# Two ends of a depthwise-convolution stage, and results kept in DRAM by block of channels

## The chip, the cores and the metric

The kernel runs on one core of a Trainium2 chip. The core has five engines that run side by side and meet through semaphores: TensorE (PE, matrix products into PSUM), VectorE (DVE), ScalarE (ACT), GpSimd (POOL) and SyncE (SP), whose work here is to issue DMAs. ScalarE and GpSimd issue DMAs too. The metric is the device time of one execution in microseconds. Every engine takes its instructions in the order in which they stand in its queue, so an instruction that waits holds up all that stand behind it.

## The reference

Two layers follow each other on x of 32 images, 96 channels and 56 by 56 pixels, in float32:

```python
# layer 0
h = conv_general_dilated(x, conv_w, (1, 1), ((3, 3), (3, 3)), feature_group_count=96) + conv_b   # 7 x 7
h = (h - mean_c(h)) * rsqrt(var_c(h) + 1e-5) * ln_g + ln_b        # over the 96 channels
h = gelu(h @ w1 + b1) @ w2 + b2                                    # 96 -> 384 -> 96
x = h * layer_scale + x
# layer 1
x = silu(conv_general_dilated(x, conv_w, (1, 1), ((2, 2), (2, 2)), feature_group_count=96) + conv_b)  # 5 x 5
dts, Bs, Cs = x_proj_w @ x
delta = softplus(dt_w @ dts + dt_b)
P = exp(cumsum(maximum(delta * A, log 1e-9)))                      # A = -exp(A_logs), along the 3136 pixels
y = sum_n(P * cumsum(delta * Bs * x / maximum(P, 1e-9)) * Cs) + x * Ds
```

## The kernel before

The work falls into four stages that follow each other: the 7x7 convolution with the sums for the norm (lines 181 to 481), the MLP (487 to 589), the 5x5 convolution (596 to 683) and the scan (691 to 972). Between stages the results lie in DRAM.

**First convolution.** There are 48 jobs of TensorE work (line 185). The first 40 take two channels each, both halves of the image rows; the last eight take four channels of one half each, four jobs for the lower half (40 to 43) and four for the upper (44 to 47). A job has an x tile of four loads (`load_x`, 224 KB each), a tile of taps of four loads (`load_taps`, from a padded table `taps1_d` in DRAM), a matrix made from the taps by one ScalarE copy (`turn`), 128 products in two PSUM tiles (`convolve`), the eviction with the bias on ScalarE and the store to `conv1_d` by ScalarE's queue (`evict`), and sums and sums of squares for the norm on VectorE, with the square on ScalarE (`add_sums`). Four x tiles, four taps tiles, three matrices, three result tiles and four PSUM tiles are in turn.

The loop at line 453 sets the order. In round n, x and taps of job n+3 are asked for, job n is convolved and evicted, its sums begin, the matrix of job n+2 is turned, and the squares of job n-1 are summed. Calls that go through `pin` keep the order of the program on their engine; calls without it are placed by a scheduler. Before, the x and taps loads and the loads of rows aren't pinned, and the scheduler has put the taps on SP two jobs ahead of the x rows (taps of job n+2 stand before x of job n). From round 2 on, one entry of the list `beside` (line 345) is done per round: `first_weights` (w1 is scaled by ln_g and centred by a product into a PSUM tile, and the bias by three more), `first_rows` four times (VectorE copies the product out of PSUM to four quarters of `w1r_t`, three copies each), `second_weights`, `scan_weights`, `scan_rows`, `turn_taps` and `second_taps` four times, the last of which stores the second convolution's table `taps2_d` by SP's queue.

In job 44 the norm of the lower half is finished (`finish_norm`: sums on VectorE, square root on ScalarE, reciprocal on VectorE) and stored to `rstd_d` by GpSimd's queue.

**MLP.** Its 28 groups are four image rows of one half of the images each. `load_rows` brings three tiles h of 128 partitions (four rows times 32 channels) by four loads each, 32 partitions per load, and a tile r (the reciprocals, the same for all channels) by four loads, all by SP's queue. `normalise` multiplies h by r on VectorE. `hidden` and `result` are the two products, with the GELU on ScalarE between them and the sum with x on VectorE after them. A finished tile of four rows and 32 channels goes to `block_d` by four stores of GpSimd's queue (line 563). `load_rows` for the first two groups is called in the convolution's round 45 (line 479).

**Second convolution.** For each of 96 channels, `load_channel` brings a tile of taps and two tiles of 120 partitions from `block_d` (30 rows times four pieces of 480 values), by SP's queue. Sixteen products per half, a SiLU on ScalarE and four copies (three on VectorE, line 660) follow, and the store to `conv2_d`.

Every DMA of the built program takes one of eight completion semaphores of its kind in turn (eight for SP and ScalarE together, eight for GpSimd), and waits until the previous DMA on that semaphore has landed.

Of the kernel before, what the change touches and what calls it, by code (L numbers as in the profile page):

```python
# [8 lines left out]
F32 = mybir.dt.float32  # L9
# [40 lines left out]
def convnext_then_scan_kernel(  # L50
# [29 lines left out]

    conv1_d = [dram.tile([128, C, HALF], F32, name=f"conv1_{h}_d") for h in range(2)]
    block_d = dram.tile([C, H, QC, B2, BI * QP], F32, name="block_d")
    conv2_d = dram.tile([C, H, B * W], F32, name="conv2_d")
    du_d = dram.tile([B * NCH, C, 2, CH], F32, name="du_d")
    rstd_d = [dram.tile([128, HALF], F32, name=f"rstd_{h}_d") for h in range(2)]
# [23 lines left out]
    def two(t):  # L111
        return t.rearrange("p (s q) -> p s q", s=2)
# [44 lines left out]
    def load_rows(n):  # L157
        h, row, p = group(n)
        for d in range(blocks):
            ht = inputs.tile([128, COLS], F32, name=f"h_{n}_{d}", tag="h", bufs=9)  # L160
            for i in range(RB):
                nc.sync.dma_start(
                    two(ht[CB * i : CB * i + CB]),
                    conv1_d[h].rearrange("(p s m) c q -> p m c s q", s=2, m=RW)[
                        p, row + i, CB * d : CB * d + CB
                    ],
                )
            hts[n, d] = ht
        rt = inputs.tile([128, COLS], F32, name=f"r_{n}", tag="r")
        rts[n] = rt  # L170
        for i in range(RB):
            at = rstd_d[h][2 * RW * p + row + i, 0:1]
            nc.sync.dma_start(
                two(rt[CB * i : CB * i + CB]),
                bass.AP(at.tensor, at.offset, [[0, CB], [RW * HALF, 2], [1, HALF]]),
            )
# [4 lines left out]
    with tc.tile_pool(name="prep", bufs=1) as prep, tc.tile_pool(name="c1", bufs=4) as pool, tc.tile_pool(  # L181
# [14 lines left out]
        def load_x(n):  # L196
            xts[n] = pool.tile([128, 2 * COLS], F32, name=f"xt1_{n}", tag="xt")
            for k, (c, h) in enumerate(jobs[n]):
                nc.sync.dma_start(
                    two(xts[n][RW * k : RW * k + RW]),  # L200
                    x[c].rearrange("(j m) q -> m j q", m=H)[h * (H - RW) : h * (H - RW) + RW],
                )

        load_x(0)

# [19 lines left out]
        for t in acc1, acc2:  # L225
            nc.vector.memset(t, 0.0)

        c2b_t = across(c2b, 128, C, "c2b_t", const)
        dtb_t = column(dtb, C, "dtb_t", const)
        g_t = column(ln_g, C, "g_t")  # L230
        lnb_t = column(ln_b, C, "lnb_t")
        b2_t = column(b2, C, "b2_t")
        ls_t = column(ls, C, "ls_t")
        ls_b = across(ls, 128, C, "ls_b")
        ds_t = column(ds, C, "ds_t")
        w1_t = prep.tile([C, F], F32, name="w1_t")
        nc.gpsimd.dma_start(w1_t, w1)
        b1_t = prep.tile([128, 3], F32, name="b1_t")
        nc.gpsimd.dma_start(b1_t, b1.rearrange("(f p) -> p f", p=128))
        nc.gpsimd.dma_start(w2_t, w2.rearrange("(f p) c -> p f c", p=128))  # L240
# [28 lines left out]
        def second_taps(k):  # L269

            for f in range(QC):
                for t in range(2):
                    j = 4 * t + (k if k < 2 else k - 4) - f + K2 // 2
                    if j in range(K2):
                        kept(nc.vector.tensor_copy,
                            pad2[:, k, RW - K2 : RW, f * 2 + t], turned[:, :, j]
                        )
            if k == QC - 1:
                nc.sync.dma_start(taps2_d, pad2)

        w1g = prep.tile([C, F], F32, name="w1g")
        held: dict = {}
# [1 line left out]
        def first_weights():  # L284

            cen = prep.tile([C, C], F32, name="cen")
            kept(nc.vector.tensor_scalar, cen, ident[:C, :C], -1.0 / C, None, ALU.add)
            kept(nc.vector.tensor_scalar, w1g, w1_t, g_t, None, ALU.mult)
            held["w1"] = bank("ps_w1")[:, 0]
            nc.tensor.matmul(held["w1"][:C, :F], lhsT=cen, rhs=w1g, start=True, stop=True)  # L290
            ps = bank("ps_b1")[:, 0]
            for f in range(3):
                nc.tensor.matmul(
                    ps[:, f : f + 1], lhsT=w1_t[:, f * 128 : (f + 1) * 128], rhs=lnb_t,
                    start=True, stop=True,
                )
            kept(nc.vector.tensor_add, b1p_t, ps[:, :3], b1_t)
# [44 lines left out]
                sel_t, ident.rearrange("p (d n) -> p d n", n=N), mybir.AxisListType.X, ALU.add  # L342
            )

        beside = [first_weights] + [lambda i=i: first_rows(i) for i in range(RB)]
        beside += [second_weights, scan_weights, scan_rows, turn_taps]
        beside += [lambda k=k: second_taps(k) for k in range(QC)]

        def load_taps(n):

            wt = pool.tile([128, RW * K1], F32, name=f"wt1_{n}", tag="wt")
            for k, (c, h) in enumerate(jobs[n]):
                at = taps1_d[c, (1 - h) * R1 * K1 : (1 - h) * R1 * K1 + 1]
                (nc.sync if n else nc.scalar).dma_start(
                    wt[RW * k : RW * k + RW],
                    bass.AP(at.tensor, at.offset, [[K1, RW], [1, RW * K1]]),
                )
            wts[n] = wt

        def turn(n):  # L360
# [31 lines left out]
        def evict(n, pss):  # L392
            job = jobs[n]
            hs = (
                pool_o.tile([128, JT, HALF], F32, name=f"hs1_{n}", tag="hs")
                if n
                else pool_o.tile([128, JT, HALF], F32, name="first", bufs=1)
            )
            c, h = jobs[n][0]
            for a in range(2):  # L400

                parts = (
                    [(hs.rearrange("p (h a) q -> p a h q", h=2)[:, a], pss[a][:, :, :HALF], c + a)]
                    if n < whole
                    else [(hs[:, 2 * a + k], pss[a][:, k, :HALF], c + 2 * a + k) for k in range(2)]
                )
                for to, ps, ch in parts:
                    pin(nc.scalar.activation(  # L408
                        to, ps, AF.Identity, bias=c1b_t[:, ch : ch + 1], scale=1.0
                    ))  # L410
            for g in range(2) if n < whole else [h]:
                cs = slice(c, c + 2) if n < whole else slice(c, c + JT)
                of = slice(2 * g, 2 * g + 2) if n < whole else slice(0, JT)
                pin(nc.scalar.dma_start(conv1_d[g][:, cs], hs[:, of]))
            return hs

        def add_sums(n, hs):
# [28 lines left out]
        for n in range(1, 3):  # L446
            load_x(n)
            load_taps(n)
        for n in range(2):
            turn(n)  # L450
        upper = whole + len(jobs[whole:]) // 2
        squares = None
        for n in range(len(jobs)):
            if n + 3 < len(jobs):
                load_x(n + 3)
                load_taps(n + 3)
            pss = convolve(n)
            norm = finish_norm(0) if n == upper else iter(())
            next(norm, None)
            hs = evict(n, pss)  # L460
            next(norm, None)
            if n == 0:
                first = hs
            if n == len(jobs) - 2:
                for d in range(blocks):
                    normalise(0, d)
            before, squares = squares, add_sums(n, hs)
            next(norm, None)
            if n + 2 < len(jobs):
# [12 lines left out]

# [4 lines left out]
    with tc.tile_pool(name="mlp_g", bufs=14) as pool_g, tc.tile_pool(  # L487
# [47 lines left out]
        def result(n, s, d):  # L535
# [24 lines left out]
                ))  # L560
            if p == 1 and s == 1:
                m = (1 - h) * QR + row
                for i in range(RB):
                    nc.gpsimd.dma_start(  # L564
                        block_d[CB * d : CB * d + CB, m + i].rearrange("c k j q -> c (k j q)"),
                        ot[CB * i : CB * i + CB].rearrange("p k q -> p (k q)"),
                    )

        parts = groups * 2
        norm = finish_norm(1)  # L570
# [25 lines left out]
    with tc.tile_pool(name="c2", bufs=3) as pool, tc.tile_pool(  # L596
# [13 lines left out]
        def load_channel(c):  # L610
# [406 lines left out]
```

## Time and profile before

| | |
|---|---|
| median of three runs | 3349.66 us (3343.58 to 3350.96) |
| profiled execution, whole | 3343.99 us |
| its span, first to last instruction | 3342.2 us |
| busy: PE, DVE, ACT, POOL | 2775.9, 2599.4, 2241.5, 1686.6 us |
| first product of the first convolution | 17.90 us |
| first product of the MLP | 387.18 us |
| first product of the second convolution | 1220.20 us |
| first product of the scan | 1572.0 us |
| DMA | 788.08 MB, 303,130 packets, mean 236 GB/s |

The span is that of one profiled execution; all times in views of the trace count from its first instruction. A row of the timeline gives start, duration, engine, source line, operation, tile written and tile read, shape and number of instructions taken together; in brackets stands how long the engine had been idle and whose end released it. "SPq" and "ACTq" rows are DMAs being issued, not DMA work. In the page's slices the span is cut in 40 parts of 83.6 us, each digit a busy share in tenths. A table of windows gives, for a stretch, the busy time of each engine, TensorE's granted clock, the busy share of the 16 DMA engines and GB/s.

### The profile page before, as it was taken

What the parts mean: (1) busy time and instruction counts of PE and PEld (TensorE: products, weight loads), DVE (VectorE), ACT (ScalarE), POOL (GpSimd) and SP (SyncE); (2) the same over time, 40 slices, a digit from 0 to 9 for tenths busy, and PEclk for the clock granted to TensorE, in tenths of its full rate; (3) what the DMA queues carried; (4) which work ended last, traced back from release to release, by engine and by line L of the source; (5) the groups of instructions that cost most, each with busy time, mean ns of one, the idle gap of its engine ahead of it and who ended that gap; (6) DMA issues with size and microseconds to landing.
All of it is one profiled execution on the core that took longest, in us unless ns stands there. A gap on an engine that the chain in (4) does not pass through costs nothing. (4 is left out here: it accounts for less than half of the span.)

```text
span 3342.2 us, 54129 instructions
## 1 busy us (share of the span) xinstructions
PE 2775.9 (83%) x21898; PEld 1064.9 (32%) x21898; DVE 2599.4 (78%) x1538; ACT 2241.5 (67%) x1963; POOL 1686.6 (50%) x815
## 2 busy tenths in 40 slices
PE   5999899999999989997677777777777777777775
PEld 2566433333333333343222222222222222222221
DVE  4888743333333349997799999999999999999998
ACT  3566543333333348786888887888888888878784
POOL 1000101010010100000899898989899998989896
PEclk8999899999999999998666666666666666666767
DMA  7899856555565459998887877878787878778773
GB/s 188 262 304 293 237 152 182 149 166 163 150 183 145 129 142 278 285 289 226 293 296 246 284 258 272 261 271 277 257 280 248 291 250 283 255 273 264 269 267 113
DMA packets 303130, 788.08 MB, mean 236 GB/s; under 512 B 125680, under 2 KB 195952, under 8 KB 278336
## 3 DMA queue, kind: packets, MB, share of 16 engines
q1 hardware_dynamic: 266832, 659.81, 62.9%
q10 hardware_dynamic: 27200, 82.59, 6.6%
q0 software_dynamic: 8848, 42.23, 4.5%
q8 instruction: 172, 2.82, 0.4%
q14 instruction: 78, 0.64, 0.1%
HBM read 543.58 MB, written 240.90 MB: 235 GB/s over the span
## 5 line engine op out<-in xcount | busy, mean ns | idle before, releaser
L815 POOL TENSOR_TENSOR rep<-rep,bt 128x1568 f32<-128x1568 f32 x192 | 674.5, 3513 | 380.4 <-DMA rep<-du_d 380.4
L844 POOL TENSOR_TENSOR hs<-hs,ct 128x1568 f32<-128x1568 f32 x191 | 669.4, 3505 | 98.6 <-DVE hs L832 87.2
L825 DVE TENSOR_TENSOR_SCAN pv<-rep,pv 128x1568 f32<-128x1568 f32 x192 | 664.4, 3461 | 40.0 <-ACT rep L811 23.0
L530 ACT ACTIVATE g<-ph,b1p_t 128x896 f32<-128x896 f32 x336 | 319.9, 1003 | 483.0 <-PE ph L520 483.0
L553 DVE SCALAR_TENSOR_TENSOR o<-po,b2r_t,x 128x224 f32<-128x224 f32 x336 | 190.8, 609 | 529.9 <-PE po L539 523.1
L564 POOL DMA_DIRECT2D block_d<-o x168 | 81.2, 490 | 727.5 <-DVE o L553 622.4
L520 PE MATMUL ph<-h,w1r_t 32*128 32x448 f32 x4032 | 430.2, 554 | 5.9 <-ACT hs L408 4.2
L743 PE MATMUL pz<-xs,wd_t 96*96 96x392 f32 x512 | 275.3, 703 | 172.6 <-ACT du L751 128.0
L539 PE MATMUL po<-g,w_t 128*32 128x448 f32 x4032 | 413.0, 543 | 0.0
L862 PE MATMUL py<-hs,sel_t 128*32 128x392 f32 x1536 | 324.9, 673 | 61.8 <-POOL hs L844 61.6
L790 PE MATMUL pk<-bn,pick_t 8*128 8x392 f32 x1024 | 289.0, 685 | 93.5 <-ACT y L871 80.4
L828 DVE SCALAR_TENSOR_TENSOR pv<-pv,rep 128x1568 f32<-128x1568 f32 x192 | 345.6, 1800 | 21.7 <-POOL rep L815 1.8
L380 PE MATMUL ps<-xt,mat 32*64 32x432 f32 (+2 forms) x6144 | 320.9, 564 | 45.2 <-ACT mat L362 38.4
L832 DVE TENSOR_TENSOR_SCAN hs<-rep,carry_h,pv 128x1568 f32<-128x1568 f32 x96 | 334.1, 3480 | 10.0
L660 DVE COPY st<-yt 28x896 f32<-28x896 f32 x288 | 323.3, 1123 | 22.7 <-ACT yt L651 12.7
L637 PE MATMUL ps<-xq,wt 128*32 128x448 f32 x3072 | 307.2, 546 | 38.6 <-DMA xq<-block_d 29.3
L832 DVE TENSOR_TENSOR_SCAN hs<-rep,pv 128x1568 f32<-128x1568 f32 x96 | 328.4, 3420 | 9.6
L810 ACT ACTIVATE rep<-rep,lift_t 128x1568 f32<-128x1568 f32 x192 | 307.6, 1602 | 6.2
L811 ACT ACTIVATE rep<-rep,lift_t 128x1568 f32<-128x1568 f32 x192 | 307.6, 1602 | 6.3
L809 ACT ACTIVATE rep<-rep,a_t 128x1568 f32<-128x1568 f32 x192 | 308.3, 1606 | 1.8 <-DMA rep<-du_d 1.4
L854 PE MATMUL py<-xs,dsm_t 96*96 96x392 f32 x512 | 299.7, 726 | 10.0 <-ACT ct L794 4.5
L520 PEld LDWEIGHTS ph<-h,w1r_t 32*128 32x128 f32 x4032 | 192.3, 185 | 245.5 <-issue 153.0
(110 smaller groups left out, 2795.6 us busy)
## 6 DMA issues: line engine op xcount, KB each, us to landing
rep<-du_d SPq DMA_DIRECT2D x191, 1568.0 KB, 8.2
du_d<-du SPq DMA_DIRECT2D x126, 588.0 KB, 9.2
xq<-block_d SPq DMA_DIRECT2D x192, 225.0 KB, 5.1
xt<-in_x_dram SPq DMA_DIRECT2D x192, 224.0 KB, 4.6
block_d<-o POOLq DMA_DIRECT2D x168, 240.0 KB, 4.9
h<-conv_d SPq DMA_DIRECT2D x336, 112.0 KB, 2.6
x<-in_x_dram SPq DMA_DIRECT2D x336, 112.0 KB, 2.5
conv_d<-st SPq DMA_DIRECT2D x96, 392.0 KB
```

The source lines that it names most:

```text
L380: nc.tensor.matmul(pss[k // 2][2 * RW * p : 2 * RW * p + 2 * RW, k % 2, :HALF].rearrange("p (i r) -> p i r", r=W2)[:, :, lo:hi], lhsT=wv[r ...
L520: pin(nc.tensor.matmul(phs[i // 2][:, i % 2, :HALF], lhsT=w1r_t[rows, d, f * 128 : (f + 1) * 128], rhs=hts[n, d][rows, s * HALF : (s + 1) ...
L530: pin(nc.scalar.activation(gt, ph[:, :, :HALF], AF.Gelu, bias=b1p_t[:, f : f + 1], scale=1.0))
L539: pin(nc.tensor.matmul(po[CB * i : CB * i + CB, :HALF], lhsT=w2_t[:, f, CB * d : CB * d + CB], rhs=gts[n, s, f, i // 2][:, i % 2], start=( ...
L660: pin(copy(st[:, :, :, :, f], yt[RW * f : RW * f + QR].rearrange("p h (b q) -> p h b q", q=QW),))
L809: pin(nc.scalar.activation(da, da, AF.Exp, scale=a_t[:, g : g + 1]))
L815: pin(nc.gpsimd.tensor_mul(ut, ut, bts[i // NG]))
L825: pin(nc.vector.tensor_tensor_scan(grown, da, zero, pv[:, last : last + 1] if q else 1.0 / EPS, ALU.mult, ALU.add))
L828: pin(nc.vector.scalar_tensor_tensor(run, in0=grown, scalar=1.0, in1=ut, op0=ALU.min, op1=ALU.mult))
L832: pin(nc.vector.tensor_tensor_scan(ht, da, run, carry_h[:, col : col + 1] if q else 0.0, ALU.mult, ALU.add))
L844: pin(nc.gpsimd.tensor_mul(ht, ht, cts[k]))
L862: pin(nc.tensor.matmul(py[g * DG : (g + 1) * DG, s, :BK], lhsT=sel_t, rhs=hss[k * NG + g][:, cols], start=False, stop=True, tile_position= ...
```

## The change

1. **w1 first.** `first_weights` and `first_rows` leave the list `beside` and are called before job 0, between the first and the second matrix. The loads they need (w1, ln_g, ln_b, b1) move to the front of GpSimd's queue, ahead of the other small loads. The product and the bias share one PSUM tile. The entries left in `beside` come five rounds earlier.
2. **Taps behind their rows.** The loads of x and of taps are pinned, so that SP has x of a job and then its taps. The taps of job 0 go by SP's queue instead of ScalarE's.
3. **The other end.** The store of `taps2_d` goes by GpSimd's queue instead of SP's. `load_rows` of the first two groups is called in rounds 44 and 45, and their r loads go by GpSimd's queue.
4. **Layout.** `conv1_d` and `block_d` are laid out by blocks of 32 channels, so that the four rows of a tile h, and the four rows of a finished block, are one contiguous piece: one load where four were, and one store where four were. The channel's loads in the second convolution then read 30 pieces of 7,680 bytes that lie 245,760 bytes apart, in place of one contiguous piece.

```diff
-    conv1_d = [dram.tile([128, C, HALF], F32, name=f"conv1_{h}_d") for h in range(2)]
-    block_d = dram.tile([C, H, QC, B2, BI * QP], F32, name="block_d")
+    conv1_d = [dram.tile([C // CB, 128, CB, HALF], F32, name=f"conv1_{h}_d") for h in range(2)]
+    block_d = dram.tile([C // CB, H, CB, QC * B * QP], F32, name="block_d")
...
-            for i in range(RB):
-                nc.sync.dma_start(
-                    two(ht[CB * i : CB * i + CB]),
-                    conv1_d[h].rearrange("(p s m) c q -> p m c s q", s=2, m=RW)[
-                        p, row + i, CB * d : CB * d + CB
-                    ],
-                )
+            rows = conv1_d[h][d].rearrange("(p s m) c q -> p (m c) s q", s=2, m=RW)
+            nc.sync.dma_start(two(ht), rows[p, CB * row : CB * (row + RB)])
...
-            nc.sync.dma_start(
+            (nc.sync if n >= 2 else nc.gpsimd).dma_start(
                 two(rt[CB * i : CB * i + CB]),
...
-                nc.sync.dma_start(
+                pin(nc.sync.dma_start(
                     two(xts[n][RW * k : RW * k + RW]),
...
-        c2b_t = across(c2b, 128, C, "c2b_t", const)
-        dtb_t = column(dtb, C, "dtb_t", const)
+        w1_t = prep.tile([C, F], F32, name="w1_t")
+        nc.gpsimd.dma_start(w1_t, w1)
         g_t = column(ln_g, C, "g_t")
         lnb_t = column(ln_b, C, "lnb_t")
+        b1_t = prep.tile([128, 3], F32, name="b1_t")
+        nc.gpsimd.dma_start(b1_t, b1.rearrange("(f p) -> p f", p=128))
...
-                nc.sync.dma_start(taps2_d, pad2)
+                nc.gpsimd.dma_start(taps2_d, pad2)
...
-            held["w1"] = bank("ps_w1")[:, 0]
+            ps = bank("ps_w1")
+            held["w1"], ps = ps[:, 0], ps[:, 1]
...
-        beside = [first_weights] + [lambda i=i: first_rows(i) for i in range(RB)]
-        beside += [second_weights, scan_weights, scan_rows, turn_taps]
+        beside = [second_weights, scan_weights, scan_rows, turn_taps]
...
-                (nc.sync if n else nc.scalar).dma_start(
+                pin(nc.sync.dma_start(
                     wt[RW * k : RW * k + RW],
...
-                cs = slice(c, c + 2) if n < whole else slice(c, c + JT)
+                d, at = divmod(c, CB)
+                cs = slice(at, at + 2) if n < whole else slice(at, at + JT)
                 of = slice(2 * g, 2 * g + 2) if n < whole else slice(0, JT)
-                pin(nc.scalar.dma_start(conv1_d[g][:, cs], hs[:, of]))
+                pin(nc.scalar.dma_start(conv1_d[g][d][:, cs], hs[:, of]))
...
-        for n in range(2):
-            turn(n)
+        turn(0)
+        first_weights()
+        for i in range(RB):
+            first_rows(i)
+        turn(1)
...
-            if n == len(jobs) - 3:
-                load_rows(0)
-                load_rows(1)
+            if n in (upper, upper + 1):
+                load_rows(n - upper)
...
-                for i in range(RB):
-                    nc.gpsimd.dma_start(
-                        block_d[CB * d : CB * d + CB, m + i].rearrange("c k j q -> c (k j q)"),
-                        ot[CB * i : CB * i + CB].rearrange("p k q -> p (k q)"),
-                    )
+                nc.gpsimd.dma_start(
+                    block_d[d, m : m + RB].rearrange("m c q -> (m c) q"),
+                    ot.rearrange("p k q -> p (k q)"),
+                )
...
-                rows = block_d[c, (H - RW + 2) * (1 - h) : (H - RW + 2) * (1 - h) + RW - 2]
+                first = (H - RW + 2) * (1 - h)
+                rows = block_d[c // CB, first : first + RW - 2, c % CB]
                 pin(nc.sync.dma_start(
                     xqs[c % len(xqs)][h][2 * QC * h : 2 * QC * h + (RW - 2) * QC],
-                    rows.rearrange("m k j q -> (m k) (j q)"),
+                    rows.rearrange("m (k q) -> m k q", k=QC),
                 ))
```

More of the change, by code (lines that the diff above doesn't have):

```diff
@@ L198, in load_x @@
             for k, (c, h) in enumerate(jobs[n]):
-                nc.sync.dma_start(
+                pin(nc.sync.dma_start(
                     two(xts[n][RW * k : RW * k + RW]),
                     x[c].rearrange("(j m) q -> m j q", m=H)[h * (H - RW) : h * (H - RW) + RW],
-                )
+                ))
         load_x(0)
@@ L234, in convnext_then_scan_kernel @@
         ls_b = across(ls, 128, C, "ls_b")
+        nc.gpsimd.dma_start(w2_t, w2.rearrange("(f p) c -> p f c", p=128))
+        c2b_t = across(c2b, 128, C, "c2b_t", const)
+        dtb_t = column(dtb, C, "dtb_t", const)
         ds_t = column(ds, C, "ds_t")
[L236 to L240, printed above, removed]
         xp_t = prep.tile([R, C], F32, name="xp_t")
@@ L288, in first_weights @@
             kept(nc.vector.tensor_scalar, w1g, w1_t, g_t, None, ALU.mult)
-            held["w1"] = bank("ps_w1")[:, 0]
+            ps = bank("ps_w1")
+            held["w1"], ps = ps[:, 0], ps[:, 1]
             nc.tensor.matmul(held["w1"][:C, :F], lhsT=cen, rhs=w1g, start=True, stop=True)
-            ps = bank("ps_b1")[:, 0]
             for f in range(3):
@@ L353, in load_taps @@
                 at = taps1_d[c, (1 - h) * R1 * K1 : (1 - h) * R1 * K1 + 1]
-                (nc.sync if n else nc.scalar).dma_start(
+                pin(nc.sync.dma_start(
                     wt[RW * k : RW * k + RW],
                     bass.AP(at.tensor, at.offset, [[K1, RW], [1, RW * K1]]),
-                )
+                ))
             wts[n] = wt
@@ L562, in result @@
                 m = (1 - h) * QR + row
-                for i in range(RB):
-                    nc.gpsimd.dma_start(
-                        block_d[CB * d : CB * d + CB, m + i].rearrange("c k j q -> c (k j q)"),
-                        ot[CB * i : CB * i + CB].rearrange("p k q -> p (k q)"),
-                    )
+                nc.gpsimd.dma_start(
+                    block_d[d, m : m + RB].rearrange("m c q -> (m c) q"),
+                    ot.rearrange("p k q -> p (k q)"),
+                )
         parts = groups * 2
```

## The prediction

> **What bounds the kernel now.** I read the page's slices first, then the table of windows at the stage borders, then TensorE's timeline in the first stage and ScalarE's at its end. The chain of what ended last lies in the scan alone (VectorE 6%, GpSimd 4%), so it says nothing of the stages that change.
>
> ```profile
> PE   5999899999999989997677777777777777777775
> DMA  7899856555565459998887877878787878778773
> ```
> ```profile
> 200.00:260.00 60.00, 59.84 (x1216) 43.43 (x1208) 57.07 (x29) 36.60 (x37) 0.00 (x0) 1.00 1.00 303
> 355.00:388.00 33.00, 18.75 (x260) 9.68 (x264) 25.96 (x24) 12.81 (x19) 0.55 (x1) 0.77 0.78 245
> 388.00:1209.00 821.00, 819.28 (x8064) 305.88 (x8056) 283.93 (x428) 327.38 (x342) 86.64 (x168) 1.00 0.53 153
> 1209.00:1558.00 349.00, 307.32 (x3076) 132.15 (x3072) 325.27 (x295) 273.64 (x193) 3.35 (x7) 0.98 0.93 279
> ```
>
> The columns of the second block are stretch, length, busy us of PE, weight loads, VectorE, ScalarE and GpSimd, then clock, DMA share and GB/s. In its best stretch (200 to 260) the first convolution has TensorE, VectorE and DMA full together: 9.4 jobs of 6.36 us at 303 GB/s. The MLP (388 to 1209) is TensorE without gaps. The second convolution is VectorE's copies (320.5 of 349 us) with DMA at 0.93. So only the first stage has time to give, at its two ends:
>
> ```profile
> 17.90 20.48 PE L380 MATMUL ps<-xt,mat 32*64 32x448 f32 x384 [17.90 <-ACT mat L362]
> 52.41 1.56 PE L290 MATMUL ps_w<-w1g,cen 96*96 96x384 f32 x2 [14.04 <-DVE w1g L259]
> 54.98 9.04 PE L380 MATMUL ps<-xt,mat 32*64 32x448 f32 x132
> 96.22 4.15 PE L380 MATMUL ps<-xt,mat 32*64 32x448 f32 x48 [2.45 <-DVE w1r_t L259]
> ...
> 361.53 8.66 PE L380 MATMUL ps<-xt,mat 32*64 32x448 f32 x128 [6.71 <-ACT mat L362]
> 373.71 9.28 PE L380 MATMUL ps<-xt,mat 32*64 32x448 f32 x128 [3.52 <-ACT mat L362]
> 387.18 6.34 PE L520 MATMUL ph<-h,w1r_t 32*128 32x448 f32 x28 [4.19 <-ACT hs L408]
> ```
> ```profile
> 15.95 1.28 ACT L362 ACT_TABLE_LOAD   x1 [15.95 <-DMA wt<-taps_d]
> ...
> 359.02 1.28 ACT L139 ACT_TABLE_LOAD   x1 [4.55 <-DMA h<-conv_d]
> 373.06 0.59 ACT L362 COPY mat<-wt 128x224 f32<-128x224 f32 x1 [9.48 <-DMA r<-rstd_d]
> ```
>
> The brackets hold the idle time before a row and what ended it. TensorE idles 63.4 us before 388: 17.9 until the first taps land, 14.0 for the folded w1, 6.1 more in jobs 4 to 8, 0.7 at job 10, 6.2 in jobs 19 to 24, 4.0 in jobs 35 to 41, 14.4 in the last two jobs and at the MLP's start. At the end ScalarE, in order, sits with its conv1 store: each DMA takes one of eight completion semaphores in turn and waits for that semaphore's previous owner, here the 19 small h loads and the r loads that wait for the norm.
>
> **What the Trainium skill says.** "DMA: Bandwidth & Descriptors", section "Issuing engines are not separate DMA queues": a transfer runs on the same 16 engines whichever queue issues it. The trace agrees: the stage stops at 303 GB/s with SP and ScalarE both issuing, so moving a store to GpSimd frees the queue, not bandwidth. The same page, "Latency and other measured facts", lists HBM row pitches: 512 KiB at full rate, 2 MiB and more slower; the new pitches here are 56 and 240 KiB, and no run here shows them. "TensorE: Matmul & The Clock Gate", section "What's actually happening": an array left idle restarts at half clock for some 3.4 us. The trace agrees: jobs after a long gap take 9.04, 8.66 and 9.28 us against 6.36, so such a gap costs about 2.5 us beyond itself.
>
> **The change, part by part.**
>
> *Head.* The job-0 taps load leaves ScalarE's queue for SP's, behind four x rows rather than beside eight. Its store has landed at 7.5 us in both (SP's and ScalarE's waits end at 7.6). Four issues take 1.8 us (the row at 7.60), and with 0.9 MB instead of 1.8 MB ahead I take 2.7 us for landing (this line's loads: 1.8 least, 4.9 median): 12.0. Table load 1.28 and copy 0.60 follow: first matmul at 13.9, **-4.0** (0 if the landing stays slow, -5 at best). The wait is new to SP: from about 2.9 to 7.6 it stands before those taps, with x of jobs 1 and 2 behind; x of job 1 then lands by some 15, and job 1 needs it at 20.7. The w1 load needs to come before that: GpSimd issues it, g, ln_b and b1 right after the memsets, at about 3.3 to 5.6; an early small load took 4.7 us (c2b, 3.27 to 8.0). So w1g is made near 9, the matmuls (2.6 us) end near 12 under the wait for the taps, and twelve copies (6.6 us) end before job 0's sums need VectorE at 22. Without that cover they cost at most 2.6. Gone: the gap **-14.0**, its 2.6 us of matmuls **-2.6**.
>
> *Held PSUM bank.* The w1 bank no longer takes one of four tiles through jobs 3 to 8: 0.38+1.08+1.07+1.10+2.45 = **-6.1**. Two slow restarts go with the gaps, 9.04 to 6.5 and 8.0 to 6.5: **-4.0**. The other weight work moves five jobs earlier, and the loads now have no pause to catch up in. VectorE has 6.1 of 6.36 us filled per job and gets 6.9 us of small copies in eight jobs; buffers for two jobs cover it. For all that I give back **+3** (0 to 9).
>
> *Order of x and taps.* Before, taps ran two jobs ahead of x on SP; now they follow their own rows. Counted from the end of job n: the store of n lands at about +6.7 (1.9 evict, 4 to 5 to land), releases the last taps DMA of job n+4, which lands by +10 to +12; ScalarE wants it at about +15 and TensorE at +19.1, three jobs on. Cover is some 4 us, so cost 0; if it goes, every job pays the excess.
>
> *Taps of the second convolution to GpSimd; h in one load.* SP stood 5.0 us for that table at 149 to 154, with x and taps behind it; then came the h loads, and TensorE lost 6.2 us plus 1.8 of slow restart (8.15 us at 160). On GpSimd the store waits for VectorE's last copy, and behind it stands only the rstd store of job 44. The bytes stay (0.79 + 0.46 MB, 4 us at 303 GB/s), so **-5** of 8 (-1 to -8). At jobs 35 to 41 the h load holds one semaphore, not four: **-1.5** of 4.0.
>
> *Tail.* From the end of job 43 (342.1): sums and norm finish on VectorE at +15.7. ScalarE's store of job 44 now waits only for a taps load, so sqrt and the next tap matrix end at +17, not +19.4. Job 46 runs 8.66 to +25.7; the store of job 45 waits for the fifth h load, about +24 (3.2 MB of h and 0.9 of store from +12, at 270 GB/s), and the last tap matrix is ready before +25.7, so job 47 follows at once and ends at +32.2. rstd lands at about +25, the four r loads now on GpSimd at about +30, and VectorE's three multiplications end at +33. Behind these r loads GpSimd has only the five block memsets, which wait for VectorE's last sums anyway (393.6 before). Evicting job 47 (2.2) opens the MLP at +34.5 instead of +45.1: **-10.6** (-4 to -14).
>
> *Stores of the blocks, channel loads.* 168 GpSimd issues of 0.49 us become 42, on an idle engine under TensorE's MLP: nothing. At the last block, three issues less (1.4 us) before the 11.04 us wait, with the same bytes on DMA: **-1** (-2 to +1). The channel loads keep 1,920-byte packets, 240 per channel, now from 7,680-byte pieces 240 KiB apart: 0.
>
> Sum: -4.0-14.0-2.6-6.1-4.0+3.0-5.0-1.5-10.6-1.0 = **-45.8**. Against the profiled execution's 3343.99 (span 3342.2) that is 3298.2; the runs' median, 3349.66, stands 5.7 higher, their lowest beside the profile. Between, I forecast **3301 us**. DMA as a check: to the end of job 45 some 93 MB pass, 2 MB by 13 us; at 300 GB/s that is 316, and my sum puts that end at 354.8-34.2 = 320.6. It fits, barely.
>
> **Rivals.**
> 1. *DMA or late taps set the pace.* For: share 1.00 at 303 GB/s, taps cover of only 4 us. Against: 200 to 260 ran without gaps. At +0.4 us in 44 jobs, 18 us come back: **3319**.
> 2. *Nearly every gap closes.* All 63.4 idle less 13.9, plus 8 of restarts and 2.6: -60, so **3287**. Against: the norm's own chain (4 us) stays.
> 3. *Slower: the channel loads by strided pieces.* Its place is the second convolution, at 0.93 DMA share. A channel there takes 3.48 us and about 3.2 of DMA work by the trace's packets (1,920 bytes: 111 ns). It decides when a channel takes 0.48 us more, which is 0.76 more of DMA work, packets of 162 ns. At 190 ns (1.19 us more work, 0.28 of it hidden) the stage grows by 87 us: 3301+87 = **3388**. Against: size and count stay, and the pitch is half of one the skill lists at full rate.
> 4. *The w1 work is not early.* If w1's load lands after the taps, job 0 waits behind it in TensorE's order; even landing at 14.8, as before, it leaves a 3 us later start: **3304**.
>
> **How the numbers follow.** Forecast and rival 4: 0.66; rival 1: 0.17; rival 2: 0.08; rival 3: 0.06, of which 0.05 end slower; no net change by a mixture: 0.03. A measurement tells about 0.2% (7 us) from none. So faster 0.92, same 0.03, slower 0.05. The low end is rival 2 (3286), the high end rival 1 with the head's and tail's poor bounds (3326).
>
> **What would show it.** First convolution matmul near 14, w1's two matmuls before it; no gap at jobs 2 to 8; no SP pause for the second taps; job 46 with a gap of about 4 us, job 47 with none; first MLP matmul near 341, first of the second convolution near 1173; the last two stages as long as before. Wrong if jobs 10 to 45 average over 6.8 us (rival 1), if the second convolution exceeds 355 us (rival 3), or if the MLP, at 4.86 us a step, waits for h.

## The result: a first stage 26 us shorter, a second convolution 50 us longer

The changed kernel takes 3368.83 us in the median (3365.04 to 3370.23, four runs), beside 3347.43 (four runs too) for the kernel before: a ratio of 1.0062, 95% interval 1.0045 to 1.008. It is slower by 0.6%, where a gain of 49 us to 3301 was forecast.

Both profiled executions, cut at the first and last matmul of each stage (job ends are counted from the first convolution's matmuls, 128 to a job):

| Stretch | Before, us | After, us | Difference | Forecast |
|---|---|---|---|---|
| to the end of job 2 | 38.38 | 38.23 | -0.2 | -4.0 |
| jobs 3 to 9 | 73.48 | 53.04 | -20.4 | -23.7 |
| jobs 10 to 45 | 242.95 | 245.16 | +2.2 | -6.5 |
| end of job 45 to the MLP's first matmul | 32.37 | 24.36 | -8.0 | -10.6 |
| MLP, first to last matmul | 821.98 | 825.33 | +3.4 | 0 |
| wait until the second convolution | 11.04 | 7.90 | -3.1 | -1.0 |
| second convolution | 334.71 | 384.55 | +49.8 | 0 |
| its end to the end of the span | 1787.30 | 1789.78 | +2.5 | 0 |
| span | 3342.2 | 3368.4 | +26.2 | -45.8 |

Each column is one execution. How far a row can vary is seen in jobs 10 to 45, which eight of the executions reported here run as the change made them: they took 240.8 to 247.3 us, so the +2.2 says only that the forecast gain of 6.5 did not come.

The table of windows of the kernel after, at the borders that answer to those shown of before (stretch, length, busy us of PE, weight loads, VectorE, ScalarE and GpSimd, clock, DMA share, GB/s):

```profile
200.00:260.00 60.00, 57.80 (x1162) 41.57 (x1154) 54.45 (x28) 36.16 (x36) 0.00 (x0) 1.00 1.00 303
336.00:361.00 25.00, 15.85 (x271) 9.04 (x264) 18.85 (x18) 12.63 (x19) 4.80 (x9) 0.83 0.91 299
361.00:1186.00 825.00, 820.95 (x8064) 306.94 (x8064) 291.48 (x434) 327.60 (x342) 30.63 (x47) 0.99 0.47 153
1186.00:1580.00 394.00, 316.19 (x3076) 132.85 (x3072) 311.45 (x295) 263.91 (x192) 0.53 (x1) 0.97 0.84 246
```

The last row is the loss. VectorE, which filled 325 of 349 us there, is now idle for a fifth of the stage, and DMA stands at 0.84 and 246 GB/s, down from 0.93 and 279. Neither of the two resources that were full before is full now.

TensorE's timeline of the kernel after, in the first stage:

```profile
10.16 1.59 PE L286 MATMUL ps_w<-w1g,cen 96*96 96x384 f32 x2 [10.16 <-DVE w1g L254]
...
17.48 20.75 PE L374 MATMUL ps<-xt,mat 32*64 32x448 f32 x384 [4.66 <-ACT mat L356]
...
49.51 9.24 PE L374 MATMUL ps<-xt,mat 32*64 32x448 f32 x128 [1.49 <-ACT hs L402]
...
341.11 8.61 PE L374 MATMUL ps<-xt,mat 32*64 32x448 f32 x128 [4.67 <-ACT mat L356]
350.06 6.60 PE L374 MATMUL ps<-xt,mat 32*64 32x448 f32 x128 [0.34 <-ACT mat L356]
360.80 5.92 PE L517 MATMUL ph<-h,w1r_t 32*128 32x448 f32 x28 [4.14 <-ACT hs L402]
370.01 3.99 PE L517 MATMUL ph<-h,w1r_t 32*128 32x448 f32 x24 [3.29 <-ACT g L527]
```

w1's matmuls stand ahead of the first job and their gap at 52 is gone. But the first convolution matmul, which waits for the first tap matrix, is hardly earlier (17.48 against 17.90), and the MLP opens at 360.80, not near 341. ScalarE's timeline of the kernel after at the stage's end:

```profile
338.60 1.28 ACT L139 ACT_TABLE_LOAD   x1 [2.60 <-DMA wt<-taps_d]
...
349.40 0.60 ACT L356 COPY mat<-wt 128x224 f32<-128x224 f32 x1 [6.25 <-DMA h<-conv_d]
...
356.95 1.70 ACT L434 ACTIVATE dt<-dt 128x1792 f32<-128x1792 f32 x1 [3.25 <-DMA r<-rstd_d]
```

The store ahead of the square root waits for a taps load as forecast (2.60 us, 4.55 before). The copy of the last tap matrix, which stood 9.48 us behind rstd loads before, now stands 6.25 us behind an h load. A wait put down to rstd is left one store later: 3.25 us, which hold up the eviction of the last job.

Where the second convolution's time went is seen on SyncE. Its timeline in the kernel before, one channel (start, length of the issue, what is issued):

```profile
1407.90 0.33 SPq L666 DMA_DIRECT2D conv_d<-st  x1
1408.32 0.52 SPq L614 DMA_DIRECT2D wt<-taps_d  x1
1408.89 2.07 SPq L625 DMA_DIRECT2D xq<-block_d  x2
```

and in the kernel after:

```profile
1410.35 0.50 SPq L663 DMA_DIRECT2D conv_d<-st  x1
1410.95 0.56 SPq L610 DMA_DIRECT2D wt<-taps_d  x1
1411.56 2.71 SPq L622 DMA_DIRECT2D xq<-block_d  x2
```

In both the issues follow each other with hardly a pause (some 0.1 us), so a channel lasts as long as SyncE takes for its four. That includes time in which an issue lasts longer than the least of its kind; this document calls it waiting for room. The second of the two channel loads went from 0.44 us in the median to 0.82, the least of the first from 0.58 to 0.85, and the store behind them, whose code is unchanged, from 0.33 to 0.50. The load's packets did not change: those of 1,920 bytes took 111 ns in both stages, and loads even land sooner (median 4.2 us, 5.1 before). The waits of the kernel before, in 320 us of the second convolution (engine, line, what for; total us, times, longest):

```profile
ACT st L660 <- DMA conv_d<-st: 57.1, 74, 2.6
...
PE ps L637 <- DMA xq<-block_d: 18.2, 31, 1.7
```

and of the kernel after, in 370 us:

```profile
ACT st L657 <- DMA conv_d<-st: 107.5, 82, 2.4
DVE st L657 <- DMA conv_d<-st: 60.8, 67, 2.0
PE ps L634 <- DMA xq<-block_d: 51.0, 56, 2.1
```

VectorE and ScalarE wait for staging tiles whose store has not landed, TensorE for channels whose load has not landed. For the loads it is the issue that is late, since they land sooner after it than before. For the stores the trace gives no landing; their packets, of 7,168 bytes, took 357 ns in the mean, 329 before.

The Trainium skill, "Perfetto Trace Analysis", section "DMA Instruction — HWDGE (DVE, Sync)", says what such a span holds: the wait for the descriptor generator, the generation and the push of the semaphore, not the movement of data; only then is the sequencer free. The trace fits: the second load's issue ends after 0.82 us, and loads land 4.2 us after their issue. How the 0.82 us divide between these parts it does not show.

### The profile page after: what moved, and what is told of

The parts are those of the page before. It is cut to its first block, busy times and chain, and to the rows that moved or that the text cites. A ratio compares the mean times of both kernels' runs of the same rounds, so it can differ in the third digit from the quotient of the medians.

```text
span 3368.4 us, 53638 instructions
## 1 busy us (share of the span) xinstructions
PE 2789.2 (83%) x21898; PEld 1069.1 (32%) x21898; DVE 2586.8 (77%) x1538; ACT 2233.3 (66%) x1963; POOL 1632.4 (48%) x698
## 5 line engine op out<-in xcount | busy, mean ns | idle before, releaser
L822 DVE TENSOR_TENSOR_SCAN pv<-rep,pv 128x1568 f32<-128x1568 f32 x192 | 664.5, 3461 | 42.9 <-ACT rep L808 26.2
L560 POOL DMA_DIRECT2D block_d<-o x42 | 22.4, 533 | 779.3 <-DVE o L550 770.6
L634 PE MATMUL ps<-xq,wt 128*32 128x448 f32 x3072 | 316.1, 558 | 76.4 <-DMA xq<-block_d 59.9
L657 DVE COPY st<-yt 28x896 f32<-28x896 f32 x288 | 310.4, 1078 | 82.0 <-DMA conv_d<-st 62.5
L825 DVE SCALAR_TENSOR_TENSOR pv<-pv,rep 128x1568 f32<-128x1568 f32 x192 | 345.6, 1800 | 21.3 <-POOL rep L812 1.4
```

Source lines behind the costliest of these rows:

```text
L634: pin(nc.tensor.matmul(ps[RW * f : RW * f + RW, h, : B * QW].rearrange("p (b q) -> p b q", q=QW), lhsT=wv[:, f, t], rhs=xv[:, :, t : t + Q ...
L657: pin(copy(st[:, :, :, :, f], yt[RW * f : RW * f + QR].rearrange("p h (b q) -> p h b q", q=QW),))
L822: pin(nc.vector.tensor_tensor_scan(grown, da, zero, pv[:, last : last + 1] if q else 1.0 / EPS, ALU.mult, ALU.add))
L825: pin(nc.vector.scalar_tensor_tensor(run, in0=grown, scalar=1.0, in1=ut, op0=ALU.min, op1=ALU.mult))
```

## Experiments: what holds up the channel loads

Theory S: a level is a count with a step, and the new layout gives the load's source three of them (30 rows 61,440 numbers apart, 4 pieces 480 apart, 480 numbers), where before rows and pieces made one level of 120 (two levels with the 480 numbers); SyncE issues that more slowly, and its queue sets the pace. Theory D is the prediction's rival 3: DRAM answers more slowly when a channel's pieces lie 240 KiB apart. First, is it the layout at all? (The four stores come back with it in this run and the next two; their lines are not shown.)

```diff
-    block_d = dram.tile([C // CB, H, CB, QC * B * QP], F32, name="block_d")
+    block_d = dram.tile([C, H, QC, B2, BI * QP], F32, name="block_d")
...
-                rows = block_d[c // CB, first : first + RW - 2, c % CB]
+                rows = block_d[c, first : first + RW - 2]
```

> The changed kernel with the result of the MLP laid out by channel again, as before the change (a channel's 120 rows are one contiguous piece, four stores for four rows); everything else stays changed. Both theories put the loss into the second convolution's channel loads, so both expect its length, first to last matmul, back at 335 us instead of 385, and the whole at 3369 - 50 = 3319 us. If the loss sat elsewhere (in the stores, or in the first stage), the stage stays near 385.

Measured: 3322.73 us, ratio to before 0.9924 (0.9908 to 0.9941); second convolution 335.5 us. The layout it is. Then the two that part the theories, levels without distance:

```diff
-    block_d = dram.tile([C // CB, H, CB, QC * B * QP], F32, name="block_d")
+    block_d = dram.tile([C, H, QC * B * QP + 64], F32, name="block_d")
...
-                rows = block_d[c // CB, first : first + RW - 2, c % CB]
+                rows = block_d[c, first : first + RW - 2, : QC * B * QP]
```

> As the run with channel rows, but each row of 7,680 bytes is followed by 256 unused bytes, so that the load's source has three levels (30 rows, 4 pieces, 480 numbers) as in the changed kernel, while all of a channel still lies within 0.45 MB. Theory S (SyncE's issue of a three-level pattern takes 0.8 us instead of 0.4, and SyncE's queue sets the pace): second convolution 380 to 390 us, whole about 3367. Theory D (DRAM: the pieces of a channel lie 240 KiB apart): 335 to 338 us, whole about 3320.

Measured: 3374.56 us, ratio 1.008 (1.0065 to 1.0095); second convolution 384.9 us. 256 bytes of padding cost as much as 240 KiB. SyncE's timeline of this run:

```profile
1410.13 0.50 SPq L664 DMA_DIRECT2D conv_d<-st  x1
1410.74 0.55 SPq L611 DMA_DIRECT2D wt<-taps_d  x1
1411.34 2.51 SPq L623 DMA_DIRECT2D xq<-block_d  x2
```

And distance without levels:

```diff
-    block_d = dram.tile([C // CB, H, CB, QC * B * QP], F32, name="block_d")
+    block_d = dram.tile([C // CB, H, QC, CB, B * QP], F32, name="block_d")
...
-                    rows.rearrange("m (k q) -> m k q", k=QC),
+                    rows.rearrange("m k q -> (m k) q"),
```

> The changed kernel with the result laid out by block, row, quarter and then channel: the 120 pieces of 1,920 bytes of a channel lie 60 KiB apart at one even pitch, so that the source has two levels but is scattered even more than in the changed kernel. Theory S: second convolution 335 to 340 us, whole about 3320. Theory D: 385 us or more, whole 3369 or more. The stores write 1,920-byte pieces instead of 7,680, under the MLP, which both expect to hide.

Measured: 3323.05 us, ratio 0.9934 (0.9919 to 0.9949); second convolution 333.7 us, although no two pieces of a channel touch. SyncE's timeline:

```profile
1406.04 0.43 SPq L623 DMA_DIRECT2D xq<-block_d  x1
1406.58 0.33 SPq L664 DMA_DIRECT2D conv_d<-st  x1
```

The second load takes 0.42 us in the median again and the store 0.33. Theory D falls: pieces 60 and 240 KiB apart both moved at 110 to 111 ns a packet. Last, a lighter queue for SyncE, with the slow pattern kept:

```diff
-            pin(nc.sync.dma_start(
+            pin(nc.gpsimd.dma_start(
                 wt,
```

> The changed kernel with one edit: in the second convolution the 96 loads of taps are issued by GpSimd, which is idle there, instead of SyncE. Theory S: SyncE is rid of 0.71 us and a 0.11 us gap in each channel of 4.01, so the stage falls until VectorE's copies (3.4 us a channel) or the transfers set the pace: 335 to 350 us, whole 3320 to 3335. Theory D: bytes and addresses on the DMA engines are the same, so 385 us and 3369 stay.

Measured: 3315.91 us, ratio 0.9904 (0.9889 to 0.9919); second convolution 329.5 us, shorter than in the kernel before. The table of windows of this run shows what is full there now:

```profile
1200.00:1510.00 310.00, 283.74 (x2904) 127.44 (x2897) 302.46 (x272) 259.45 (x183) 89.50 (x90) 1.00 0.92 288
```

VectorE's copies fill 302 of 310 us. This version beats both kernels; it is the base of what follows. It is not as clean as the two runs before it: issued by GpSimd, the same bytes of taps went in a quarter as many packets (4,096 bytes in place of 1,024). And no run tells SyncE's own time from that of whatever makes the descriptors behind its queue, since the load left both.

The number of levels is not the whole price. The taps load in both kernels has a source of three levels too (32 by 4 by 256 numbers, 128 pieces), and SyncE issued it in 0.52 us before the change and 0.56 after, not 0.82. So the runs show that this load costs 0.4 us more once its rows and pieces no longer fold; what sets the size of that is open.

Did SyncE bind the stage before the change too? The same edit in the kernel before:

> The kernel before with one edit: the 96 loads of taps of the second convolution are issued by GpSimd. Asks whether SyncE's queue was already the bound there before the change. Its four issues and gaps fill all of the 3.49 us of a channel, but the least times of the issues add up to 2.2 us; the rest is waiting for room. If that wait is for the transfers and VectorE's copies: 329 to 335 us instead of 334.7, whole 3342 to 3348. If SyncE itself bound it, 3.49 - 0.65 leaves VectorE's 3.36 us a channel: 323 us, whole 3336.

Measured: 3341.98 us, ratio 0.9986 (0.9978 to 0.9993); second convolution 328.0 us, 6.7 less, of which the wait ahead of it took back 2.5. That is 1 us below the range for "SyncE waits for others" and 5 above the value for "SyncE binds": the queue was at most a small part of the bound, beside VectorE and the transfers, although its issues stood back to back there too. The sums show how little room there was. The least times of four issues and gaps make 2.1 us before and 2.8 after; the means fill the channel in both (3.49 and 4.0). So 1.4 and 1.2 us of a channel went to waiting for room, and this waiting hardly shrank when the issues grew. Why not is not settled; that issues and waiting alternate in one queue, and so add, is argued, not shown.

## Experiments: where the first stage's gain went

Theory B, the prediction's rival 1: the transfers' bandwidth sets jobs 10 to 45. Theory L: taps that come late in the new order. The order undone:

```diff
-                pin(nc.sync.dma_start(
+                nc.sync.dma_start(
                     wt[RW * k : RW * k + RW],
```

(the x loads likewise)

> The kernel of the last run (taps of the second convolution issued by GpSimd) with one part of the change undone: x and tap loads of the first convolution are no longer held in written order, so that tap loads go up to two jobs ahead of x on SyncE again. Theory B (the transfers' bandwidth sets the pace of jobs 10 to 45: 72.2 MB in 242 us): they take 241 to 248 us as before the edit, whole 3311 to 3321. Theory L (taps that come late in the new order set it): 6.5 us a job, 234 us, whole about 3308 or less.

Measured: 3314.07 us, ratio 0.9902 (0.9887 to 0.9917); jobs 10 to 45 in 243.8 us (242.4 in the base). The order costs nothing, as forecast. Then the bytes. This kernel leaves out one of the two stores of each of the first 40 jobs and lets the MLP read the other half's results in their place:

```diff
-            for g in range(2) if n < whole else [h]:
+            for g in range(1) if n < whole else [h]:
```

> The same base with half of the first convolution's stores left out (the lower halves of the results are never stored, and the MLP reads the upper halves in their place; the output isn't the reference's). Loads, taps order and all compute stay. That takes 0.46 MB of 2.0 from each job. Theory B: TensorE and VectorE set the pace, 6.25 to 6.4 us a job, jobs 10 to 45 in 225 to 230 us instead of 242, and the idle gaps before tap matrices vanish. Theory L: the order of taps behind x is unchanged, so 240 us or more stay.

Measured: jobs 10 to 45 in 224.9 us, 6.25 a job; whole 3290.78, ratio 0.9833 (0.9813 to 0.9852). The table of windows of this run:

```profile
100.00:300.00 200.00, 200.00 (x4116) 167.16 (x4106) 191.75 (x99) 132.81 (x135) 0.00 (x0) 1.00 0.94 253
```

and of the base:

```profile
100.00:300.00 200.00, 193.65 (x3798) 133.22 (x3790) 179.96 (x94) 117.69 (x119) 0.53 (x1) 0.99 0.99 300
```

With about a fifth of the bytes gone (57.2 MB in jobs 10 to 45, 72.2 in the base), TensorE runs 200 us without a gap; with all of them DMA is at 0.99 and TensorE has gaps. Theory B holds against theory L; that half of the store issues went with the bytes is answered by the next run. The DMA share alone would not have told: it is 0.94 where nothing waits. If bytes pace the stage, do fewer and larger packets help?

```diff
-            for g in range(2) if n < whole else [h]:
-                d, at = divmod(c, CB)
...
+            if 0 < n < wide:
+                pin(nc.scalar.dma_start(
+                    both_d[d][:, at : at + 2].rearrange("p c h q -> p (c h) q"), hs
+                ))
+                return hs
```

> The same base; for channels 0 to 63 the first convolution's two halves lie side by side in DRAM and in SBUF, so that jobs 1 to 31 store with packets of 7,168 bytes instead of 3,584 (128 instead of 256 a job, one issue instead of two). Theory B: packets of 7,168 bytes took 283 to 294 ns in the last jobs, those of 3,584 159 ns in the stores; a job's transfers shrink from 256 x 159 to 128 x 290 ns, over 16 engines 0.22 us, so 31 jobs give 7 us: jobs 10 to 45 in 237 us, whole 3309. If transfers are paid by bytes alone: 242 to 247 us and 3316.

Measured: 3318.32 us, ratio 0.9919 (0.9904 to 0.9933); jobs 10 to 45 in 246.7 us. My expectation was wrong: of these, jobs 10 to 31, which have the wide stores, took 149.6 us, 150.5 in the base and 137.1 with the stores left out. A job has one store issue here as it has in that run, so it was the bytes that counted there and not the issues. From 90 to 230 us the stores' packets of 7,168 bytes took 307 ns (321 for two of the base's), but the x loads' packets of 3,584 went from 196 to 225 ns beside them. DMA share was 1.01 at 292 GB/s from 100 to 230 us, against 0.99 at 301 in the base: halving a stream's packets bought no rate. With the stores left out, the same x packets took 223 ns as well, at 250 GB/s, so a packet's time is not a fixed price that could be summed up in advance.

w1's preparation put back beside the jobs:

```diff
-        first_weights()
-        for i in range(RB):
-            first_rows(i)
...
+        beside = [first_weights] + [lambda i=i: first_rows(i) for i in range(RB)]
```

> The same base with w1's preparation back beside the jobs (its two matmuls after job 2, its copies in the following ones) while its loads stay early. By the prediction's sum, 14.0 + 2.6 + 6.1 us come back and stay: job 9 ends 23 us later, whole 3339. By theory B, part of what is lost early is caught up, since the bytes are ahead while TensorE waits: as in the kernel before, 1.7 MB fewer are left for jobs 10 to 45, which is 6 us; so whole 3330 to 3335. Since w1 and the scale are loaded early now, the gap can also be much shorter than the 14 us that were seen: then within 10 us of 3316.

Measured: 3331.59 us, ratio 0.9947 (0.993 to 0.9964), 16 us above the base. TensorE's timeline of this run:

```profile
50.78 1.57 PE L286 MATMUL ps_w<-w1g,cen 96*96 96x384 f32 x2 [11.89 <-DVE w1g L254]
...
95.48 8.04 PE L375 MATMUL ps<-xt,mat 32*64 32x448 f32 x124 [2.47 <-DVE w1r_t L254]
```

Even with w1 loaded early the gap is 11.9 us: VectorE scales w1 only behind the sums of the first jobs, so it is the place in its order, not the load. Job 9 ends at 111.1 (89.8 in the base). Of these 21.3 us nothing was caught up in the profiled executions: jobs 10 to 45 took 244.7 us (242.4), though 1.6 MB less moved in them, and the span is 24.5 us longer. (The medians differ by less because the base's profile is its fastest run and this one's its slowest.) So early w1 work is worth its full gap, and the bytes alone do not give the time of jobs 10 to 45; what else holds them is open.

The tail, in two parts. The h and rstd loads of both groups after job 45:

```diff
-            if n in (upper, upper + 1):
-                load_rows(n - upper)
+            if n == len(jobs) - 3:
+                load_rows(0)
+                load_rows(1)
```

> The same base with the loads of h and rstd for the first two groups both back after job 45, as before the change (h still in one load of four rows, rstd still on GpSimd). By the prediction the store of job 44 then waits again for an h load, and the MLP opens 45 us after the end of job 43 instead of 36: whole 3324. Rival: it is the rstd loads on SyncE that held ScalarE's stores, and they stay on GpSimd here: 36 us and 3316.

Measured: 3314.41 us, ratio 0.9904 (0.9889 to 0.9919); the MLP opens 35.9 us after job 43. The place of the loads is worth nothing. The rstd loads:

```diff
-            (nc.sync if n >= 2 else nc.gpsimd).dma_start(
+            nc.sync.dma_start(
```

> The changed kernel with the taps of the second convolution on GpSimd (the base, 3316 us) and the rstd loads of the first two groups back on SyncE. If these loads held ScalarE's stores in the kernel before: the MLP opens 45 us after the end of job 43 instead of 36, whole 3324. If it was the number of h loads (four to a tile before, one now): 36 us and 3316 stay.

Measured: 42.9 us after job 43, but 3319.15 us, ratio 0.9917 (0.9902 to 0.9931). TensorE's timeline:

```profile
357.61 8.21 PE L374 MATMUL ps<-xt,mat 32*64 32x448 f32 x128 [5.74 <-ACT mat L356]
368.12 4.94 PE L517 MATMUL ph<-h,w1r_t 32*128 32x448 f32 x28 [2.30 <-ACT hs L402]
374.75 6.89 PE L517 MATMUL ph<-h,w1r_t 32*128 32x448 f32 x48 [1.69 <-ACT g L527]
```

Most of the tail's gain is the rstd loads' move: without it the last job waits 5.74 us (0.34 in the changed kernel), and 6.6 of 8 us return. But the MLP then takes 822.7 us instead of 826.2 in the base: an MLP that opens earlier stands longer for its first activations (the 3.29 us at 370.01 above), so half is given back.

The head, with GpSimd's later loads held until the first taps have landed:

```diff
+        load_taps(0)
+        hold = prep.tile([1, 1], F32, name="hold")
+        pin(nc.gpsimd.tensor_copy(hold, wts[0][:1, :1]))
         b2_t = column(b2, C, "b2_t")
```

> The same base; GpSimd's loads after w1, scale, ln_b and b1 wait until the first job's taps have landed. If those loads were in the way of the first taps: first convolution matmul at 14 us instead of 16 to 18. If the taps' landing is slow without them: 16 to 18. By theory B the whole stays at 3310 to 3318 in both cases, since the same bytes are only moved behind.

Measured: first convolution matmul at 15.01; whole 3314.17, ratio 0.9912 (0.9894 to 0.993). SyncE's last issue of these taps ended at 11.5 here and ScalarE's wait for them 1.6 us later; in the changed kernel 10.9 and 15.5, 4.6 us. But the eleven other runs with the new head spread widely, the first matmul at 15.99 to 18.38 and the taps' landing 2.4 to 5.2 us after the issue, and the base itself is the best of them (15.99, 2.4). That some of GpSimd's loads were in the way is therefore likely, not shown. The wait for the store of the taps was not cured: SyncE could issue at 9.8 here, at 9.2 in the changed kernel and at 7.6 before. The whole did not move, as expected.

## Why the prediction was wrong

**The step that failed** is the last sentence of the part by part: "The channel loads keep 1,920-byte packets ... : 0". Size, count and time of the packets did stay (111 ns). What changed was the issue, which was never costed: per channel 0.38 us more on the second load (medians), 0.27 on the first (least times) and 0.17 on the store behind them, in a queue whose means already filled the channel. It measured 49.8 us, 0.52 a channel. The trace of before held all that was needed to ask: the second stage read as VectorE at 325 of 349 us and DMA at 0.93, and I stopped there without adding up SyncE's issues, since the page doesn't count them as busy. That the form of a load matters could be seen there (0.52 us for the taps load's three levels, 0.33 for the store), but not the price of this one, so it should have been bounded from both sides: nothing, or say a doubling of the 0.44 us issue, which on a full queue is an estimate of 2 x 0.4 us in 96 channels, 77 us.

**Rival 3** had the place and the sign, and the mark that it set (the stage over 355 us) was passed, at 384.55. Its mechanism is refuted: the load's packets stayed at 111 ns in the mean and never came near 162. That its mark was passed is luck, since the 0.06 rested on a pitch that is harmless. The note on row pitches that the prediction cited (the Trainium skill, "DMA: Bandwidth & Descriptors", section "Latency and other measured facts") begins at 512 KiB, where it gives 207 GB/s beside 214 that it calls full: nearly the full rate, not quite. It says nothing of 60 and 240 KiB, which the runs show to be harmless here, and has no bearing on the issue.

**Rival 1** came true as well by its mark: jobs 10 to 45 average 6.81 us, just over its mark of 6.8. The mark was a narrow one: before the change the same jobs averaged 6.75. The prediction saw that its sum left 316 us of transfers in 320.6 and wrote "it fits, barely"; job 45 ended at 336.4. Its two terms for gaps in these jobs (-6.5; by a count of 128 matmuls to a job these are jobs 17 to 22 and 33 to 40, not 19 to 24 and 35 to 41) came to +2.2: the gap of 3.39 us behind the second taps is gone, and others stand in its place. Of the two causes that rival 1 joined, bandwidth is shown by the run with half the stores, and the order of the taps costs nothing. Rival 1's price of 18 us is twice what was lost (8.7). That 3301, its 18 and the 50 of the second convolution make 3369 is a coincidence; by the table the forecast of -45.8 was missed by 72.0: 49.8 in the second convolution, 8.7 in jobs 10 to 45, 3.8 at the head, 3.3 in jobs 3 to 9, 2.6 at the tail, 3.4 in the MLP and 2.5 at the end, less 2.1 at the wait ahead of the second convolution.

**Right**: w1's gap, its matmuls and the held bank (-20.4 for jobs 3 to 9 against -23.7 with the give-back); no cost of the order of x and taps; no SyncE pause for the second taps; the gap of job 46 (4.67, some 4 forecast) and hardly any of job 47 (0.34); slow restarts after gaps (9.24 and 8.61 us against 6.6). They last longer than the 3.4 us at half clock that the prediction quotes with "the trace agrees": the kernel before's job of 9.28 us at 373.71 has a mean granted clock of 0.67, by estimate 6.1 us at half clock.

**Sizes that were off**: the head (-0.4 to the first matmul instead of -4.0), where the store of the taps let SyncE issue at 9.2 and not 7.6, and 2.7 us for a landing, chosen nearer the least (1.8) than the median (4.9) of its line, became 4.6; the tail (-8.0 instead of -10.6, and 3.4 given back in the MLP), where the gain is mostly the rstd loads' move; the wait ahead of the second convolution (-3.1 instead of -1.0: 7.9 to 8.7 us in the runs with one store for four rows after the change, 11.6 to 12.0 in the three with four stores). No gap at jobs 2 to 8 was also wrong: 0.64, 1.22, 1.49 and 0.75 us remain.

## What to carry to other kernels

Before a DMA's layout is changed, write down both sides' levels as the instruction will carry them, and add up the issues of its queue per step, which no busy share shows. A queue that issues back to back is a suspect, not yet a bound: before the change, relieving it gave 7 us, after it 55. A layout that saves stores can cost more at the load; an even pitch, which lets rows and pieces fold into one level, or an idle queue for one of the loads, cured it here. And in a stage at 300 GB/s and DMA share 0.99, gaps that were closed inside it came back as others: of what was tried, only fewer bytes shortened it.

## What the runs showed of the hardware

- As the second of two such loads, 120 pieces of 1,920 bytes took SyncE 0.42 to 0.44 us to issue (medians) with a source of two levels and 0.82 to 0.83 us with three, whatever the distance of the pieces (256 bytes of padding or 240 KiB); the next issue behind it, unchanged, went from 0.33 to 0.50 us. Another load of three levels, 128 pieces of 1,024 bytes, took 0.52 to 0.56 us.
- Pieces 60 KiB and 240 KiB apart moved as fast as contiguous ones: 110 to 111 ns for 1,920 bytes.
- Halving the number of one stream's packets raised the time of the other stream's (3,584 bytes: 196 to 225 ns) when the packets were doubled in size, at 292 GB/s instead of 301, and as well when half of them were left out (223 ns, at 250 GB/s).
- A DMA share of 0.94 at 253 GB/s stood beside a TensorE without a gap for 200 us.
